# A causal mask folded into the row maximum on VectorE, cosine tables on ScalarE's queue, and the first rows normalized on ScalarE

## The chip, the cores and the metric

The kernel runs on one core of a Trainium2 chip. The metric is the device time of one execution in microseconds; the figure given is the median of three runs. Each core has five engines that run side by side and wait for each other by semaphores: TensorE (matmuls and transposes), VectorE, ScalarE, GpSimd, and SyncE, which here only issues transfers.

## The reference

One transformer block in float32 over 2048 rows of 1024 columns: attention with 16 heads of 64 columns and rotary positions, then a gated feed-forward part of 2752 columns whose weights are 4-bit codes with a scale per block of 64. Each part is wrapped in layer norms on both sides:

```python
x = x + layernorm(attn(layernorm(x), Wq, Wk, Wv, Wo))
x = x + layernorm(ffn(layernorm(x), gate, up, down))

# in attn, for each head
q, k = rotary(h @ Wq), rotary(h @ Wk)
logits = q @ k.T
logits = where(causal, logits, -1e9) / sqrt(64)
out = softmax(logits) @ (h @ Wv)

# in ffn
down(silu(gate(h)) * up(h))
```

## The kernel before

**Precision.** A float32 operand of a matmul is carried as a high part and a low part. `split` (L119) makes them: ScalarE casts the high part (L120), VectorE subtracts it from the source for the low part (L121). A product of two split operands is three matmuls (`mm3`, L114 to L116).

**First stage (make_x, prep_w, qkv).** `make_x` (L188) loads 128 rows of x at a time, takes the row statistics on VectorE and GpSimd (L126 to L137), normalizes the rows on VectorE (L195), transposes them on TensorE (L151) and splits the result. Four such row blocks make one block of 512 rows, of which there are four (c = 0 to 3). `prep_w` loads a slice of 128 columns of a projection's weights and splits it: ScalarE casts (L178), and for the first two slices GpSimd scales and subtracts (L183, L184). `qkv(m, c, ...)` (L211) projects row block c onto column slice m, which holds two heads. It loads the cosine and sine table of the block (`tab`, L214), makes 24 matmuls each for query, key and value, and takes the result out of its PSUM bank with a ScalarE copy (L223, L233). A query or key then goes through the rotary step: a shuffle (L235) and a product with the cosines (L236) on VectorE, a product with the sines (L237) and a sum (L238) on GpSimd, a split (L120, L121) and a store. A value is transposed (L226), cast and subtracted in two halves (tile `vo`, L230) and stored. The first two slices for all four row blocks, eight calls, form the ramp: they have `ramp=True`; with the transposes of x they are what TensorE does before attention starts. The tables live in the SBUF slot `f4`, of which there are four and which weight tiles, rotary results and value tiles share.

**Attention (scores, weighted).** For each head and each block J of 512 queries, `scores` (L244) goes through four sub-blocks j of 128 query rows. For each it takes the keys in tiles of up to 512 columns. A tile of scores is two matmuls into one of three PSUM banks named S (L260, L262). The last tile of each sub-block holds the diagonal: it is 128, 256, 384 or 512 columns wide, and only its last 128 columns are cut by the mask. There a third matmul (L264) adds the mask: identity times a triangle of -1e9, both in bfloat16. VectorE then takes the negated row maximum (L266), and ScalarE the exponential with that as its bias, with the row sums (L267). Over the whole kernel there are 640 tiles, 256 of them with the diagonal. After every second sub-block the sums are combined on VectorE (L272 to L284), and GpSimd scales the probabilities (L289). `weighted` (L292) transposes the probabilities (L299), splits them and multiplies them by the values (L303, L304). The projections of the later heads (`group`, L363) are placed between the attention work of the earlier ones.

**The rest.** The output projection (L445 to L447), the first residual with its layer norms (`residual`, L450, whose `normalize` at L144 is a ScalarE activation), the gated feed-forward with weights looked up from the codes, and a down projection done in seven half-size products with a last layer norm (`finish`, L682).

**What sets the order.** A planner sorts the program's instructions onto the engines by its own estimate of their durations and by priorities; `early` (L323) raises the priority of the first weights and of the x blocks, and `pace` ties projections to points in the attention work. Each engine then runs its list strictly in order. A transfer is issued by an instruction in the list of the engine whose queue is used: `load` is SyncE's. It carries one of eight completion semaphores in turn, and waits until the transfer that used the same one before has landed, beside its own data waits. The PSUM banks are one F, three S, three T and one O.

Of the kernel before, what the change touches and what calls it, by code (L numbers as in the profile page):

```python
# [10 lines left out]
F32 = mybir.dt.float32  # L11
FR = mybir.dt.float32r
BF = mybir.dt.bfloat16
# [11 lines left out]
P = 128  # L25
# [32 lines left out]
def block_kernel(ctx, tc, x, wq, wk, wv, wo, gu_codes, gu_scales, d_codes, d_scales, cos_sin, out):  # L58
# [15 lines left out]
    def slot(tag, shape, dtype, name):  # L74
        assert int(np.prod(shape[1:])) * 4 <= SLOTS[tag][1] * 1024, (tag, shape)
        return sb.tile(shape, dtype, tag=tag, name=name, bufs=SLOTS[tag][0])
# [9 lines left out]

    ident = const.tile([P, P], F32, name="ident")
    make_identity(nc, ident)
    ident_b = const.tile([P, P], BF, name="ident_b")
    V.tensor_copy(ident_b, ident)  # L90
    mask_f = slot("t2", [P, P], F32, "mask_f")
    G.memset(mask_f, 0.0)

    G.affine_select(out=mask_f, in_=mask_f, compare_op=ALU.is_ge, fill=MASK, base=0, pattern=[[-1, P]], channel_multiplier=1)
    mask_b = const.tile([P, P], BF, name="mask_b")
    V.tensor_copy(mask_b, mask_f)
    nhalf = const.tile([P, 1], F32, name="nhalf")
    G.memset(nhalf, -0.5)
# [41 lines left out]
    def halves(row):  # L140
        return row[:, :512], row[:, 512:]
# [46 lines left out]
    def make_x(c):  # L188
        tiles = [slot(("pa", "xc", "hd", "xc")[c], [P, 2, 2, 512], FR, "xr") for _ in range(4)]
        for t in range(4):  # L190
            r = (4 * c + t) * P
            xt = slot("hd" if c == 0 or t == 3 else "pw", [P, E], F32, "xt")
            load(xt, x[r : r + P, :])
            mean, rs, _ = ln_stats(halves(xt))
            V.tensor_scalar(xt, xt, mean, rs, ALU.subtract, ALU.mult)  # L195
            transposed(xt, tiles, slice(t * P, (t + 1) * P))
        for kp in range(4):
            load(xd[c][:, kp], f32(tiles[kp]))
        return tiles
# [11 lines left out]
    def qkv(m, c, ws, xs, ramp=False, pace=None):  # L211
        cs = slice(c * 512, (c + 1) * 512)
        tab = slot("f4", [P, 2, 512], F32, "tab")
        load(tab, cos_sin[:, :, cs])  # L214
        for n, w in enumerate(ws):
            o = bank("S" if ramp and n != 1 else "F", "qkv")
            for k in range(KE):
                mm = mm3(o, w[k], xs[k // 2][:, :, k % 2, :], k == 0, k == KE - 1)
                if k == 0 and pace:
                    pace(mm, n)  # L220
            t1 = slot("t2", [P, 512], F32, "t1")
            if n == 2:
                A.copy(t1, o)  # L223
                pv = bank("F", "pv").rearrange("p (t n) -> p t n", t=4)
                for t in range(4):
                    T.transpose(pv[:, t, :], t1[:, t * P : (t + 1) * P], ident)  # L226
                vo = slot("f4", [P, 4, 2, 2, D], FR, "vo")
                src = pv.rearrange("p t (a d) -> p t a d", a=2)
                for a in range(2):
                    split(vo[:, :, a, 0, :], vo[:, :, a, 1, :], src[:, :, a, :])  # L230
                load(vs[m][cs].rearrange("(t p) a n -> p t (a n)", p=P), f32(vo.rearrange("p t a l d -> p t (a l d)")))
            else:
                A.copy(t1, o)  # L233
                sh = slot("t2", [P, 512], F32, "sh")
                V.stream_shuffle(sh, t1, [i ^ 1 for i in range(32)])  # L235
                V.tensor_tensor(t1, t1, tab[:, 0, :], ALU.mult)  # L236
                G.tensor_tensor(sh, sh, tab[:, 1, :], ALU.mult)  # L237
                G.tensor_tensor(t1, t1, sh, ALU.add)  # L238
                hl = slot("f4", [P, 2, 512], FR, "hl")
                split(hl[:, 0, :], hl[:, 1, :], t1)  # L240
                load((qs, ks)[n][m][:, :, cs], f32(hl))


    def scores(J, q, k, anchors):  # L244
# [3 lines left out]
        for j in range(4):  # L248
# [5 lines left out]
            for i in range(nh):  # L254
# [4 lines left out]
                s = bank("S", "s")[:, : e - b]  # L259
                mm = T.matmul(s, lhsT=q[:, 0, j * P : (j + 1) * P], rhs=k[:, b:e], start=True, stop=False)  # L260
                anchors.append(((anchors[-1][0] if anchors else 0) + e - b, mm))
                T.matmul(s, lhsT=q[:, 1, j * P : (j + 1) * P], rhs=k[:, b:e], start=False, stop=not diag)  # L262
                if diag:
                    T.matmul(s[:, e - b - P :], lhsT=ident_b, rhs=mask_b, start=False, stop=True)  # L264
                mx = mxs[:, j % BATCH, i : i + 1]
                V.tensor_reduce(mx, s, AX.X, ALU.max, negate=True)  # L266
                A.activation(prob[i][:, j, : e - b], s, AF.Exp, bias=mx, accum_out=sums[:, j % BATCH, i : i + 1])  # L267
            if j % BATCH < BATCH - 1:
                continue
            rc = small.tile([P, BATCH, 4], F32, tag="rc", name="rc")[:, :, :nh]  # L270
# [401 lines left out]
            t = slot(tag, [P, 4, 512], F32, name)  # L672
            quarter.setdefault(name, []).extend([t[:, i] for i in range(4)])

    early_stats = {}

    def stats_of(name, r):
        st = small.tile([P, 2, 6], F32, tag=f"st_{name}{r}", name="st", bufs=1)
        V.bn_stats(st[:, 0, :], quarter[name][r])
        early_stats[name, r] = st  # L680

    def finish(r, lower, known, fresh, xt):  # L682

        t = 8 * (r // 4) + 4 * lower + r % 4
        load(xt, x1d[t * P : (t + 1) * P, :])
        st = early_stats[known, r]
        known, fresh = quarter[known][r], quarter[fresh][r]
        V.bn_stats(st[:, 1, :], fresh)
        _, rs, nb = ln_rest(st)
        a, b = (slice(512, E), slice(0, 512)) if lower else (slice(0, 512), slice(512, E))  # L690
        A.activation(xt[:, b], xt[:, b], AF.Identity, bias=nb)
        A.activation(known, known, AF.Identity, bias=nb, scale=rs)
# [98 lines left out]
```

## Time and profile before

| what | us |
|---|---|
| median of 3 runs (3069.14 to 3074.55) | 3069.32 |
| the profiled execution, whole | 3075.66 |
| its span in the trace | 3073.8 |
| L264, mask matmuls, 256, busy | 59.8 |
| L266, row maxima, 640, busy | 380.0 |
| L267, exponentials, 640, busy | 400.9 |
| L236 and L237 waiting for a cosine table | 103.3 |

The busy times of a line are sums over its instructions; those of TensorE overlap each other, because a matmul starts before the one ahead of it has ended. The granted TensorE clock was 0.982 over the execution. In the lines of the profile that follow, each row has an engine, a source line, an operation, the tile written and the tile read, and the shapes. In the time line the first two numbers are the start and the length in us, and the bracket holds the idle time of the engine ahead of the instruction with what ended it. In the table of stages each engine has its busy time in the stretch. In the list of groups the numbers after the count are the busy time in us and the mean in ns, and after the second bar the idle time ahead. In the list of waits they are the total in us, the count and the longest.

### The profile page before, as it was taken

To read this page: it belongs to the slowest core of one execution; us is meant where nothing else is said; L and a number is where in the kernel's file an instruction comes from. 1 tells how busy PE (TensorE), PEld (TensorE's weight loads), DVE (VectorE), ACT (ScalarE), POOL (GpSimd) and SP (SyncE) were. 2 spreads that over 40 slices of the span, in tenths; PEclk is the share of its full clock that TensorE was granted. 3 is DMA by queue.
4 is the path that set the end of the run, shared out by engine and by line. 5 is a ranking of instruction groups with operands and counts; after the bars stand their busy time and mean duration, and the time that the engine had idled before them with its cause. 6 is when DMAs were issued, how large, how long until landed. Compare 5 with 4: busy or idle time off the path is not lost.

```text
span 3073.8 us, 42810 instructions
## 1 busy us (share of the span) xinstructions
PE 2958.1 (96%) x14424; PEld 2426.6 (79%) x14424; DVE 2045.6 (67%) x3920; ACT 1700.1 (55%) x3565; POOL 960.4 (31%) x1055
## 2 busy tenths in 40 slices
PE   7979999999999999999989999999999999999998
PEld 6868888787777787777778788888888888788886
DVE  7556778777777777777565577766666677344347
ACT  3246667676666666666554466555555566332234
POOL 5334444344434343445323112222112223100034
PEclk9989999999999999999999999999999999999999
DMA  8776665747656558463346444344334444644446
GB/s 307 259 223 219 225 217 170 221 151 194 188 182 186 152 199 260 132 198 108 114 152 209 138 143 148 132 136 142 120 133 137 136 153 148 237 140 151 147 141 229
DMA packets 271739, 536.02 MB, mean 174 GB/s; under 512 B 22944, under 2 KB 113056, under 8 KB 255648
## 3 DMA queue, kind: packets, MB, share of 16 engines
q1 hardware_dynamic: 271520, 533.29, 53.8%
q8 instruction: 114, 1.87, 0.2%
q14 instruction: 105, 0.86, 0.1%
HBM read 371.98 MB, written 161.22 MB: 173 GB/s over the span
## 4 chain that ended last, share of the span: by engine, by line
PE 83%; DMA 8%; DVE 4%; ACT 2%; issue 1%; POOL 1%; SPq 1%; POOLq 0%; ACTq 0%; DVEq 0%
PE bk L114 14%; PE bk L115 14%; PE bk L116 14%; PE pt L299 6%; PE qkv L114 6%; PE qkv L115 5%; PE qkv L116 5%; PE o L304 4%; PE s L260 3%; PE o L303 3%; PE s L262 3%; DMA wf<-in_wq 1%; PE pj L445 1%; PE pj L447 1%; PE pj L446 1%
## 5 line engine op out<-in xcount | busy, mean ns | idle before, releaser
L115 PE MATMUL bk<-x,wt 128*128 128x512 f32 x1376 | 536.1, 390 | 0.0
L116 PE MATMUL bk<-x,wt 128*128 128x512 f32 x1376 | 535.8, 389 | 0.0
L114 PE MATMUL bk<-x,wt 128*128 128x512 f32 x1376 | 534.5, 390 | 0.9 <-ACT wt L120 0.9
L289 POOL TENSOR_SCALAR prob<-prob,rc 128x512 f32<-128x512 f32 (+3 forms) x640 | 405.4, 654 | 407.5 <-DVE rc L284 238.8
L267 ACT ACTIVATE prob<-s,mxs 128x512 f32<-128x512 f32 (+3 forms) x640 | 400.9, 629 | 159.1 <-DVE mxs L266 144.8
L121 DVE TENSOR_TENSOR pw<-pt,pw 128x512 fp32r<-128x512 f32 (+3 forms) x640 | 377.4, 602 | 131.2 <-ACT pw L120 129.5
L266 DVE TENSOR_REDUCE mxs<-s 128x1 f32<-128x512 f32 (+3 forms) x640 | 380.0, 602 | 100.5 <-PE s L262 60.2
L506 ACT ACTIVATE ln<-cs,bias 128x512 f32<-128x512 f32 x520 | 359.7, 716 | 109.4 <-DVE m L513 23.0
L120 ACT CAST pw<-pt 128x512 fp32r<-128x512 f32 (+3 forms) x640 | 323.1, 525 | 164.2 <-PE pt L299 134.9
L299 PE MATMUL pt<-ident,prob 128*128 128x128 f32 x2176 | 346.5, 276 | 3.2 <-DVE pw L121 3.0
L299 PEld LDWEIGHTS pt<-ident,prob 128*128 128x128 f32 x2176 | 267.9, 142 | 57.3 <-issue 4.4
L260 PE MATMUL s<-k,q 128*128 128x512 f32 (+3 forms) x640 | 268.7, 420 | 38.1 <-ACT prob L267 36.2
L114 PEld LDWEIGHTS bk<-x,wt 128*128 128x128 f32 x1376 | 258.8, 188 | 55.4 <-ACT wt L120 1.7
L116 PEld LDWEIGHTS bk<-x,wt 128*128 128x128 f32 x1376 | 258.5, 188 | 54.1 <-DVE wt L121 0.5
L115 PEld LDWEIGHTS bk<-x,wt 128*128 128x128 f32 x1376 | 258.6, 188 | 53.7
L304 PE MATMUL o<-pw,v 128*128 128x512 f32 (+3 forms) x640 | 250.3, 393 | 5.3 <-DVE pw L121 4.7
L303 PE MATMUL o<-pw,v 128*128 128x512 f32 (+3 forms) x640 | 246.7, 386 | 4.6 <-ACT pw L120 3.7
L114 PE MATMUL qkv<-xc,w 128*128 128x512 f32 x576 | 237.0, 411 | 13.6 <-ACT w L178 9.1
L114 PE MATMUL bk<-bt,at 128*128 128x512 f32 (+1 forms) x616 | 242.1, 395 | 4.3 <-ACT in L574 4.1
L115 PE MATMUL bk<-bt,at 128*128 128x512 f32 (+1 forms) x616 | 240.7, 391 | 0.0
L116 PE MATMUL bk<-bt,at 128*128 128x512 f32 (+1 forms) x616 | 239.8, 391 | 0.0
L262 PE MATMUL s<-k,q 128*128 128x512 f32 (+3 forms) x640 | 238.6, 374 | 0.0
(145 smaller groups left out, 5478.9 us busy)
## 6 DMA issues: line engine op xcount, KB each, us to landing
xc<-xd SPq DMA_DIRECT2D x96, 1024.0 KB, 8.9
q<-qs SPq DMA_DIRECT2D x128, 256.0 KB, 7.0
ast<-S SPq DMA_DIRECT2D x44, 512.0 KB, 4.0
cs<-in_gu_scales SPq DMA_DIRECT2D x172, 128.0 KB, 3.2
cs<-in_gu_codes SPq DMA_DIRECT2D x86, 256.0 KB, 2.9
A<-in SPq DMA_DIRECT2D x66, 256.0 KB, 2.1
S<-in SPq DMA_DIRECT2D x66, 256.0 KB, 3.1
ast<-A SPq DMA_DIRECT2D x33, 512.0 KB, 4.4
```

Of the source, the lines that this page charges most:

```text
L114: r = T.matmul(o, lhsT=w[:, 0], rhs=xx[:, 0], start=first, stop=False)
L115: T.matmul(o, lhsT=w[:, 0], rhs=xx[:, 1], start=False, stop=False)
L116: T.matmul(o, lhsT=w[:, 1], rhs=xx[:, 0], start=False, stop=last)
L121: V.tensor_tensor(lo, src, f32(hi), ALU.subtract)
L260: mm = T.matmul(s, lhsT=q[:, 0, j * P : (j + 1) * P], rhs=k[:, b:e], start=True, stop=False)
L266: V.tensor_reduce(mx, s, AX.X, ALU.max, negate=True)
L267: A.activation(prob[i][:, j, : e - b], s, AF.Exp, bias=mx, accum_out=sums[:, j % BATCH, i : i + 1])
L289: G.tensor_scalar(p, p, rc[:, jj % BATCH, i : i + 1], 0.0, ALU.mult, ALU.add)
L299: T.transpose(pt[:, j * P : (j + 1) * P], prob[kb // 4][:, j, kb % 4 * P : (kb % 4 + 1) * P], ident)
L303: T.matmul(o[:, cs], lhsT=v[:, kb, :], rhs=pw[:, 0, cs], start=kb == 0, stop=False)
L304: T.matmul(o[:, cs], lhsT=v[:, kb, :], rhs=pw[:, 1, cs], start=False, stop=kb == nk - 1)
L506: A.activation(ln, c8, AF.Prelu, bias=bias_of[ab], scale=ab[0], alpha=ab[2])
```

## The change

Three things change in the work, and one in where results are kept.

- The mask matmul of a diagonal tile goes. In its place one VectorE operation adds a mask of the tile's whole width to the scores, negates the sum, writes it back to the bank, and takes the minimum of the row, which is the negated maximum. The exponential of such a tile then has a scale of -1. The mask is 512 columns wide, and a tile of width w uses its last w columns; the bfloat16 identity is no longer needed.
- The eight cosine table loads of the ramp are issued on ScalarE's queue and not on SyncE's.
- The four row blocks of c = 0 are normalized by a ScalarE activation (L144 in the code before) and not on VectorE.
- The row statistics of the last stage lie in one tile for all rows, and not in one tile for each; the operations are the same.

```diff
-    ident_b = const.tile([P, P], BF, name="ident_b")
-    V.tensor_copy(ident_b, ident)
-    mask_f = slot("t2", [P, P], F32, "mask_f")
+    mask_f = slot("t2", [P, 512], F32, "mask_f")
     G.memset(mask_f, 0.0)
 
-    G.affine_select(out=mask_f, in_=mask_f, compare_op=ALU.is_ge, fill=MASK, base=0, pattern=[[-1, P]], channel_multiplier=1)
-    mask_b = const.tile([P, P], BF, name="mask_b")
+    G.affine_select(out=mask_f, in_=mask_f, compare_op=ALU.is_ge, fill=MASK, base=384, pattern=[[-1, 512]], channel_multiplier=1)
+    mask_b = const.tile([P, 512], BF, name="mask_b")
     V.tensor_copy(mask_b, mask_f)
...
-            mean, rs, _ = ln_stats(halves(xt))
-            V.tensor_scalar(xt, xt, mean, rs, ALU.subtract, ALU.mult)
+            stats = ln_stats(halves(xt))
+            if c == 0:
+                normalize(xt, xt, stats)
+            else:
+                V.tensor_scalar(xt, xt, stats[0], stats[1], ALU.subtract, ALU.mult)
...
-        load(tab, cos_sin[:, :, cs])
+        (A.dma_start if ramp else load)(tab, cos_sin[:, :, cs])
...
-                T.matmul(s, lhsT=q[:, 1, j * P : (j + 1) * P], rhs=k[:, b:e], start=False, stop=not diag)
+                T.matmul(s, lhsT=q[:, 1, j * P : (j + 1) * P], rhs=k[:, b:e], start=False, stop=True)
+                mx = mxs[:, j % BATCH, i : i + 1]
                 if diag:
-                    T.matmul(s[:, e - b - P :], lhsT=ident_b, rhs=mask_b, start=False, stop=True)
-                mx = mxs[:, j % BATCH, i : i + 1]
-                V.tensor_reduce(mx, s, AX.X, ALU.max, negate=True)
-                A.activation(prob[i][:, j, : e - b], s, AF.Exp, bias=mx, accum_out=sums[:, j % BATCH, i : i + 1])
+
+                    V.tensor_tensor_reduce(s, s, mask_b[:, 512 - (e - b) :], -1.0, -MASK, ALU.add, ALU.min, mx)
+                else:
+                    V.tensor_reduce(mx, s, AX.X, ALU.max, negate=True)
+                sign = -1.0 if diag else 1.0
+                A.activation(prob[i][:, j, : e - b], s, AF.Exp, bias=mx, scale=sign, accum_out=sums[:, j % BATCH, i : i + 1])
...
-    early_stats = {}
+
+    parts_st = small.tile([P, 8, 3, 6], F32, tag="parts_st", name="parts_st", bufs=1)
 
     def stats_of(name, r):
-        st = small.tile([P, 2, 6], F32, tag=f"st_{name}{r}", name="st", bufs=1)
-        V.bn_stats(st[:, 0, :], quarter[name][r])
-        early_stats[name, r] = st
+        V.bn_stats(parts_st[:, r, 0 if name == "c" else 2], quarter[name][r])
...
-        st = early_stats[known, r]
-        V.bn_stats(st[:, 1, :], fresh)
-        _, rs, nb = ln_rest(st)
+        V.bn_stats(parts_st[:, r, 1], fresh)
+        _, rs, nb = ln_rest(parts_st[:, r, lower : lower + 2])
```

## The prediction

> **What bounds the kernel now.** I read the busy shares first, then the table by stage, then the time line and the waits where the stage table shows TensorE idle.
>
> ```profile
> PE 2958.1 (96%) x14424; PEld 2426.6 (79%) x14424; DVE 2045.6 (67%) x3920; ACT 1700.1 (55%) x3565; POOL 960.4 (31%) x1055
> ```
> ```profile
> core 0: us, PE busy (x) PEld busy (x) DVE busy (x) ACT busy (x) POOL busy (x), PEclk, DMA share, GB/s
> 0.00:25.00 25.00, 7.82 (x30) 5.84 (x31) 19.79 (x53) 11.15 (x26) 16.76 (x30) 1.00 1.00 308
> 80.00:160.00 80.00, 80.00 (x381) 66.49 (x380) 37.64 (x80) 20.78 (x49) 29.91 (x22) 1.00 0.71 249
> 160.00:240.00 80.00, 61.88 (x301) 49.60 (x300) 45.61 (x105) 40.43 (x108) 30.72 (x34) 0.87 0.78 237
> 400.00:700.00 300.00, 294.06 (x1631) 241.99 (x1630) 230.59 (x524) 204.28 (x536) 126.09 (x171) 0.98 0.58 183
> 1000.00:1300.00 300.00, 289.91 (x1597) 237.41 (x1596) 224.69 (x515) 199.45 (x528) 121.85 (x169) 0.98 0.59 186
> ```
>
> TensorE is the bound, in the attention stage too: 294 of 300 us, with VectorE at 230.6 of 300 (77%). The holes are in the first 25 us (7.82 busy) and between 160 and 240 (18 us idle, granted clock 0.87). TensorE's order from about 1660 us on is the same before and after the change, so only what comes ahead of it is in question. The hole after 160 us, in the time line:
>
> ```profile
> 166.23 10.85 SPq L321 DMA_DIRECT2D q<-qs  x4
> 177.78 0.62 SPq L214 DMA_DIRECT2D tab<-in_cos_sin  x1
> 187.74 0.69 DVE L236 TENSOR_TENSOR t<-t,tab 128x512 f32<-128x512 f32 x1 [18.14 <-DMA tab<-in_cos_sin]
> 188.34 1.15 DVE L266 TENSOR_REDUCE mxs<-s 128x1 f32<-128x384 f32 x2
> 189.66 0.79 PE L260 MATMUL s<-k,q 128*128 128x512 f32 x1 [13.98 <-ACT prob L267]
> ```
>
> The eighth cosine table waits on SyncE's queue behind four query loads; VectorE's rotary product (L236) waits 18.14 us for it; the row maxima stand behind that product in VectorE's order, the exponentials behind the maxima, and TensorE waits 13.98 us for a score bank.
>
> **The mask matmul (L264) goes.** Its price is not its busy time:
>
> ```profile
> 1398.81 0.34 PE L262 MATMUL s<-k,q 128*128 128x384 f32 x1
> 1398.99 0.23 PE L264 MATMUL s<-mask_b,ident_b 128*128 128x128 bf16 x1
> 1399.03 0.31 PE L304 MATMUL o<-pw,v 128*128 128x128 f32 x1
> ```
>
> By row it lasts 0.234 us, and 256 x 0.234 = 59.8 us; but the next matmul starts 0.04 us after it. TensorE is freed of 256 x 0.04 = 10.2 us. Bounds: nothing (where TensorE waits anyway) to 10.2. TensorE is over 96% busy through most of the stage, so I take -10.2.
>
> **What VectorE takes on.** 256 of the 640 row maxima (L266) become an addition with a minimum reduction that also writes the negated, masked scores back to the bank, each followed by a second instruction that reads the accumulator out (the built program has both, 256 times). No row of the trace writes PSUM from VectorE or reads its accumulator. The nearest rows:
>
> ```profile
> L266 DVE TENSOR_REDUCE mxs<-s 128x1 f32<-128x512 f32 x448 | 303.3, 682 | 71.6 <-PE s L262 60.2 <-PE s L264 9.1
> L121 DVE TENSOR_TENSOR pw<-pt,pw 128x512 fp32r<-128x512 f32 x435 | 292.1, 682 | 95.3 <-ACT pw L120 94.1
> L267 ACT ACTIVATION_READ_ACCUMULATOR prob<-s,mxs 128x1 f32 x640 | 129.3, 202 | 0.0
> L137 DVE TENSOR_SCALAR nb<-mv,rs 128x1 f32<-128x1 f32 x6 | 1.2, 205 | 1.0 <-POOL rs L135 0.9
> ```
>
> A two-operand operation from a bank costs what the reduction costs (682 ns each at 512 columns), so the main instruction adds nothing at the low end; at the high end, writing the bank halves its rate, and it costs as much again (mean reduction over the four widths 679, 547, 415 and 282 ns: 0.48 us). I take nothing: the L121 row is the same form but for the place of its output. The read-out is between 0.10 us (ScalarE's lasts 202 ns, but half of it lies inside the activation before) and 0.205 us (L137, a one-column operation on VectorE); I take 0.15: 256 x 0.15 = 38 us of VectorE over the 1350 us from the first to the last of them, 2.8 points on 77%. Here a rule speaks against the change: the Trainium skill, "VectorE: DVE Perf Modes", sections "Two Vector instructions with no wait between them" and "Rules for kernel authors", says that an operation with an accumulator output is two instructions, and that one should save VectorE instructions, since each pays a fixed part. Its fixed part of 58 to 151 cycles at 0.96 GHz would make 0.06 to 0.16 us, an estimate from that page of 15 to 40 us; by the rows it is 26 to 52. Either fits under TensorE as long as VectorE is not the bound.
>
> What is exposed is latency. Who waits:
>
> ```profile
> PE s L260 <- ACT prob L267: 36.2, 18, 14.0
> ACT prob L267 <- DVE mxs L266: 144.8, 172, 13.9
> ```
>
> TensorE waits 18 times for an exponential, one of them the 14 us above. Three score banks lie between, and 256/640 = 0.4 of the tiles are diagonal: 17 x 3 x 0.4 x 0.15 = 3.1 us. I take +3.1. ScalarE's exponential only gets a scale of -1, which costs nothing.
>
> **The cosine tables on ScalarE's queue.** Eight loads leave SyncE. In the changed order each stands between the two halves of a value cast (L120, vo), and each waits for the transfers that used its completion semaphores before; while it waits, ScalarE is held. The first seven change nothing: from 40 to 160 us TensorE is 100% busy with tables arriving late, and ScalarE has 59 of 80 us to spare, against eight issues of 0.57 to 1.55 us on SyncE's row. The eighth decides. The half cast ahead of it is at 166.4. The issue then waits for a query load issued near 162.6, whose median landing is 7.9 us: 170.5. The table takes a median 9.7 us: 180.2. From landing to the matmul took 2.0 us (187.65 to 189.66): 182.2. That is 189.66 - 182.2 = 7.5 us earlier. Behind the waiting issue on ScalarE stand the first exponential and the other half cast, which frees the single F bank for the next key projection (168.6 in the trace): up to 3 us of new wait inside the same stretch. It also moves two masked maxima ahead of the rotary product on VectorE, which helps. Bounds: nothing (the next late thing is the second head's query load, held by TensorE itself) to 14 us, and a few more for the clock of 0.87. I take -7.5. The Trainium skill, "Trainium Kernel Development and Optimization", section "Key Constraints", has it that loads from other engines' queues run on the same DMA engines and save only the time to issue. By that rule the gain is 0.6 us, one issue, and the sum below is 6.9 us worse; by the row the table stood 10.85 us behind the four query loads, which waited for TensorE and not for bandwidth. I go by the row.
>
> **The first rows on ScalarE.** Four normalizations leave VectorE (L195, 0.8 to 1.6 us each) for ScalarE (L144, 1.24 us each at 128x1024, elsewhere in the trace). VectorE is 19.8 of 25 us busy there, ScalarE 11.2. But in the changed order ScalarE does the four, then six weight casts, and the last casts of the first row blocks come after the weight casts of the second group, whose wv load reaches ScalarE at 24.45. Four casts of 0.37 us later the last quarter of the first x tile is there: 24.45 + 1.15 + 1.5 = 27.1, where TensorE's first projection starts at 24.35 now. Some eight transposes are then already done (8 x 0.11 = 0.9). I take +1.5, between -2.5 (VectorE's two normalizations on the chain, 1.42 and 1.12 us, go) and +3.
>
> **The rest** costs nothing: a mask of 512 columns is built on GpSimd and cast on VectorE before the first row arrives (VectorE idles 2.38 us there; without it, about 1 us); the statistics of the last stage are the same count of instructions in one tile.
>
> **Sum**, against the profiled execution's own 3075.66 us (span 3073.8, 1.86 around it): -10.2 + 3.1 - 7.5 + 1.5 = -13.1, giving 3062.6. That execution is 6.3 us above the median of the runs, 3069.32, so the median should come to 3056. A planner that lays out the order from its own costs reorders all that comes ahead of 1660 us; for that I allow 6 us either way.
>
> **Rivals.**
> 1. *VectorE becomes the bound.* Place: the end of each of the 64 chunks (16 heads x 4 row blocks), where the last diagonal tile, its exponential, the reciprocal and GpSimd's scaling follow in series. If the main instruction runs at half rate, a tile costs 0.48 + 0.2 = 0.68 us more, VectorE rises by 256 x 0.68 = 174 us, to 90% of the stage, and one such tile exposed per chunk is 64 x 0.68 = 43.5 us. With the other terms (-10.2 - 7.5 + 1.5) the median is 3096.6; half exposed, 3075. It decides, against the 16.2 us gained, from 0.25 us exposed per chunk. For it: 172 waits of ScalarE for the maxima. Against: only 16.3 us of TensorE's waits for exponentials lie between 400 and 1300 us.
> 2. *The table was hidden anyway, or ScalarE is held.* The wait goes over to the second head's loads, or ScalarE's held queue gives the 7.5 back: -10.2 + 3.1 + 1.5 = -5.6, median 3063.7, no change that can be told. For it: loads behind the table were themselves held. Against: in the profile nothing but the table ends VectorE's 18.14 us.
> 3. *The mask is not worth 10 us*, since another engine ends each stall: the table's gain alone, -7.5 + 3.1 + 1.5 = -2.9, median 3066.4. Against it: the 96% and more.
>
> **From these to the numbers.** A measurement tells 0.2% (6.1 us) from no change: below 3063.2 is faster, above 3075.4 slower. The sum holds, with its spread: 0.58. Rivals 2 and 3, ending within 0.2%: 0.20. Rival 1, and ScalarE held long enough in the first stage, ending above: 0.22. The range reaches down to 3037 (the whole 14 us and the clock with it, the head 2.5 us better, the planner's 6) and up to 3083, which leaves out the outer part of rival 1. The likeliest case's own range is 3040 to 3063.
>
> **What would show it.** Right: no 14 us wait of L260 near 175 us, table landing near 180; the new VectorE instruction within 0.05 us of the reduction it replaces at each width, its read-out 0.1 to 0.2; VectorE near 80% in 400 to 700 and TensorE still above 97%; a first projection near 27 us. Wrong: the new instruction near 1.3 us at 512 columns, TensorE's waits for exponentials well above 40 us in total, or waits of TensorE for value casts behind ScalarE's loads.

## The result, and the profile after

| | before | after |
|---|---|---|
| median of 4 runs each (of before, the three given above and a fourth), us | 3071.94 (3069.14 to 3075.65) | 3042.42 (3042.17 to 3048.39) |
| ratio, with its 95% interval | 1 | 0.9913 (0.9893 to 0.9932) |
| the profiled execution, whole, us | 3075.66 | 3042.64 |
| its span in the trace, us | 3073.8 | 3040.9 |
| start of the first score matmul, us | 167.4 | 169.7 |
| start of the first score matmul of the last tile (the 1279th of 1280), us | 1515.4 | 1488.3 |
| start of the feed-forward part, us | 1680.7 | 1653.5 |

The changed kernel is 29.5 us faster by the medians. The two profiled executions differ by 33.0 us, and 27.2 of these are there when the feed-forward part starts. The rest lies in the part whose order the change doesn't touch; it takes 1387 to 1393 us in the traces of all the kernels here, with or without the mask matmul.

Line numbers have moved by a few: score matmuls are L261 and L263 now, the new operation is L267, the row maximum of the other tiles L269, the exponential L271, the transposes of the probabilities L303, the table load L215, the cosine product L237, the normalization on ScalarE L142.

The first two parts of the page of the changed kernel: the busy shares of the engines, and from the table of stages three of the stretches that were shown of before (busy time of each engine, then granted clock, DMA share and GB/s).

```profile
PE 2924.4 (96%) x14168; PEld 2411.7 (79%) x14168; DVE 2031.0 (67%) x4171; ACT 1698.5 (56%) x3569; POOL 955.7 (31%) x1055
```
```profile
core 0: us, PE busy (x) PEld busy (x) DVE busy (x) ACT busy (x) POOL busy (x), PEclk, DMA share, GB/s
0.00:25.00 25.00, 6.14 (x24) 4.57 (x24) 17.25 (x47) 14.87 (x26) 17.30 (x32) 1.00 1.01 315
160.00:240.00 80.00, 73.78 (x341) 59.08 (x340) 52.94 (x139) 47.73 (x127) 32.92 (x40) 0.89 0.84 267
400.00:700.00 300.00, 292.65 (x1611) 244.72 (x1610) 232.83 (x599) 208.46 (x552) 131.96 (x181) 0.99 0.61 190
```

The hole after 160 us has shrunk from 18.1 us of idle TensorE to 6.2. In the attention stage nothing has changed hands: TensorE is 292.7 of 300 us busy where it was 294.1, and VectorE 232.8 where it was 230.6, but more of the work is done in those 300 us. The first 25 us are worse (6.14 busy against 7.82).

The new VectorE operation, from the list of groups (after the bar: busy us, mean ns of one; after the second bar: idle time ahead). The second row is the read-out, the last is the reduction that it is to be held against:

```profile
L267 DVE CUSTOM_DVE_ANT_0 s<-s,mask_b 128x512 f32<-128x512 f32 x64 | 44.1, 689 | 4.9 <-PE s L263 3.4 <-ACT pw L118 1.2
L267 DVE DVE_READ_ACCUMULATOR2_ANT mxs<- 128x1 f32 x256 | 35.6, 139 | 0.0
L267 DVE CUSTOM_DVE_ANT_0 s<-s,mask_b 128x384 f32<-128x384 f32 x64 | 35.6, 556 | 5.3 <-PE s L263 4.6 <-ACT prob L271 0.2
L269 DVE TENSOR_REDUCE mxs<-s 128x1 f32<-128x512 f32 x384 | 260.8, 681 | 59.9 <-PE s L263 58.7
```

Writing the bank costs next to nothing (689 ns against 681), and the read-out 139 ns, with no idle time of VectorE ahead of any of the 256.

The eighth cosine table and the product that needs it, in the time line, and TensorE's waits for exponentials over the whole execution (total us, times, longest):

```profile
170.69 0.55 ACTq L215 DMA_DIRECT2D tab<-in_cos_sin  x1
...
181.50 0.69 DVE L237 TENSOR_TENSOR t<-t,tab 128x512 f32<-128x512 f32 x1 [5.86 <-DMA tab<-in_cos_sin]
```
```profile
PE s L261 <- ACT prob L271: 18.8, 29, 2.3
```

The table is asked for at 170.69 (177.78 before) and used at 181.50 (187.74 before); VectorE's wait for it went from 18.14 us to 5.86. The 14 us wait of TensorE is gone, and the longest is 2.3. There are more short ones: 29 for 18.8 us, where before 17 short ones made 22.2.

The first stage shows the cost of the third part of the change:

```profile
12.39 1.11 PE L149 MATMUL pt<-ident,xt 128*128 128x128 f32 x4 [0.50 <-ACT xt L142]
13.63 1.24 ACT L142 ACTIVATE xt<-xt,nb,rs 128x1024 f32<-128x1024 f32 x1
...
24.18 1.15 ACT L176 ACTIVATE w<-wf 128x512 fp32r<-128x512 f32 x2 [0.36 <-DMA wf<-in_wv]
26.44 2.79 PE L149 MATMUL pt<-ident,xt 128*128 128x128 f32 x12 [3.31 <-DVE xr L119]
28.88 1.63 PE L112 MATMUL qkv<-xr,w 128*128 128x512 f32 x3
```

The weight casts (L176) end at about 25.3, and the first projection (L112) starts at 28.88. It was 24.35 before. By the first score matmul 2.3 us of that 4.5 are left.

### The profile page after: what moved, and what is told of

Same layout as the page of the kernel before. It is cut to its first block, busy times and chain, and to the rows that moved or that the text cites. A ratio compares the mean times of both kernels' runs of the same rounds, so it can differ in the third digit from the quotient of the medians.

```text
span 3040.9 us, 42530 instructions
## 1 busy us (share of the span) xinstructions
PE 2924.4 (96%) x14168; PEld 2411.7 (79%) x14168; DVE 2031.0 (67%) x4171; ACT 1698.5 (56%) x3569; POOL 955.7 (31%) x1055
## 3 DMA queue, kind: packets, MB, share of 16 engines
q1 hardware_dynamic: 269344, 529.10, 53.5%
## 4 chain that ended last, share of the span: by engine, by line
PE 79%; DMA 9%; DVE 5%; ACT 3%; issue 2%; POOL 1%; SPq 1%; POOLq 0%; ACTq 0%; DVEq 0%
PE bk L112 14%; PE bk L113 14%; PE bk L114 14%; PE pt L303 6%; PE qkv L112 5%; PE qkv L114 5%; PE qkv L113 5%; PE o L308 4%; PE o L307 3%; PE s L261 3%; PE s L263 3%; DMA wf<-in_wq 2%; DMA q<-qs 1%; PE pj L451 1%; PE pj L449 1%
## 5 line engine op out<-in xcount | busy, mean ns | idle before, releaser
L112 PE MATMUL bk<-x,wt 128*128 128x512 f32 x1376 | 533.7, 389 | 1.0 <-ACT wt L118 1.0
L271 ACT ACTIVATE prob<-s,mxs 128x512 f32<-128x512 f32 (+3 forms) x640 | 402.1, 632 | 148.8 <-DVE mxs L269 92.1
L119 DVE TENSOR_TENSOR pw<-pt,pw 128x512 fp32r<-128x512 f32 (+3 forms) x640 | 378.4, 601 | 122.3 <-ACT pw L118 120.5
L303 PE MATMUL pt<-ident,prob 128*128 128x128 f32 x2176 | 345.8, 275 | 7.2 <-DVE pw L119 5.9
L303 PEld LDWEIGHTS pt<-ident,prob 128*128 128x128 f32 x2176 | 268.2, 142 | 61.7 <-issue 7.5
L112 PEld LDWEIGHTS bk<-x,wt 128*128 128x128 f32 x1376 | 258.2, 188 | 55.4 <-ACT wt L118 1.8
L269 DVE TENSOR_REDUCE mxs<-s 128x1 f32<-128x512 f32 x384 | 260.8, 681 | 59.9 <-PE s L263 58.7
L113 PEld LDWEIGHTS bk<-x,wt 128*128 128x128 f32 x1376 | 258.3, 188 | 53.5
L261 PE MATMUL s<-k,q 128*128 128x512 f32 (+3 forms) x640 | 266.2, 417 | 22.4 <-ACT prob L271 18.8
L112 PE MATMUL bk<-bt,at 128*128 128x512 f32 (+1 forms) x616 | 241.0, 393 | 3.7 <-ACT in L578 3.3
L112 PE MATMUL qkv<-xc,w 128*128 128x512 f32 x576 | 231.3, 402 | 13.3 <-ACT w L176 7.3
L263 PE MATMUL s<-k,q 128*128 128x512 f32 (+3 forms) x640 | 237.2, 373 | 0.0
```

The costliest lines, as they stand in the source:

```text
L112: r = T.matmul(o, lhsT=w[:, 0], rhs=xx[:, 0], start=first, stop=False)
L113: T.matmul(o, lhsT=w[:, 0], rhs=xx[:, 1], start=False, stop=False)
L119: V.tensor_tensor(lo, src, f32(hi), ALU.subtract)
L271: A.activation(prob[i][:, j, : e - b], s, AF.Exp, bias=mx, scale=sign, accum_out=sums[:, j % BATCH, i : i + 1])
L303: T.transpose(pt[:, j * P : (j + 1) * P], prob[kb // 4][:, j, kb % 4 * P : (kb % 4 + 1) * P], ident)
```

## The experiments

My theory after reading the result was that the mask matmul is worth about three times what I gave it. The rivals: the planner's new order is what is faster, the table's gain is larger than it looks, or VectorE took over something cheaply that was dear on TensorE. In all that follows a us figure that compares kernels of different chips is a difference of ratios to the kernel before, times 3073. "The attention stretch" is the time from the start of the 127th score matmul to that of the 1279th, in the profiled execution. It holds the same scores in every kernel, with 230 of the 256 diagonal tiles, and without the mask 6100 to 6125 matmuls (6100 before, 6104 after), as the order moves some of the other work over its ends.

### The three parts, one at a time

Each part alone on the kernel before, and the second and third together. The table alone:

```diff
-        load(tab, cos_sin[:, :, cs])
+        (A.dma_start if ramp else load)(tab, cos_sin[:, :, cs])
```

> The kernel before with the ramp's eight cosine loads on ScalarE's queue and nothing else. TensorE's order is the old one from its 764th instruction to the 803rd and from there to the end, so the planner takes no part. If the table's wait was worth what the milestones of the two traces show (12 us between the ramp's end and the 32nd score tile), the median falls by 12 us to about 3059. If the forecast's term was right, by 7.5 to about 3063. If the wait only moves on to the second head's loads, there is no change.

Measured: 3068.41 us, ratio 0.9982 (0.9975 to 0.9989), 5.4 us faster. The forecast's term was -7.5. In the time line of this kernel the table is used at 182.26, but another wait has come up:

```profile
173.41 0.55 ACTq L214 DMA_DIRECT2D tab<-in_cos_sin  x1
174.00 0.37 ACT L120 CAST vo<-pv 128x256 fp32r<-128x256 f32 x1 [6.57 <-DMA k<-ks]
174.40 0.42 DVE L121 TENSOR_TENSOR vo<-pv,vo 128x256 fp32r<-128x256 f32 x1 [5.65 <-ACT vo L120]
174.97 0.77 PE L114 MATMUL qkv<-xr,w 128*128 128x512 f32 x1 [6.19 <-DVE vo L121]
...
182.26 0.69 DVE L236 TENSOR_TENSOR t<-t,tab 128x512 f32<-128x512 f32 x1 [6.30 <-DMA tab<-in_cos_sin]
```

This is the hold of the second rival: ScalarE idles 6.57 us until a key load has landed, the half cast of the values stands behind the table's issue, and TensorE waits 6.19 us for it. In the kernel with the whole change that wait isn't there (its longest in 160 to 200 us is 2.9).

The first rows on ScalarE alone:

```diff
-            mean, rs, _ = ln_stats(halves(xt))
-            V.tensor_scalar(xt, xt, mean, rs, ALU.subtract, ALU.mult)
+            stats = ln_stats(halves(xt))
+            if c == 0:
+                normalize(xt, xt, stats)
+            else:
+                V.tensor_scalar(xt, xt, stats[0], stats[1], ALU.subtract, ALU.mult)
```

> The kernel before with the first four row blocks normalized on ScalarE and nothing else. Parts theory: the first score tile comes 3 us later (2.7 in the traces) and nothing else moves, so +3 us. Planner theory: the order of all that comes ahead of the output projection is new, and the time moves by up to 10 us either way with the cold spells of the clock.

Measured: 3075.86 us, ratio 1.0011 (1.0001 to 1.0022): 3.4 us slower by the ratio, 2.1 by the medians. The first projection starts at 29.20, the first score matmul at 169.3 against 167.4.

The mask alone, that is the changed kernel with the other two parts undone (the last stage's statistics stay in one tile; the lines of the mask's edit that matter):

```diff
...
-                T.matmul(s, lhsT=q[:, 1, j * P : (j + 1) * P], rhs=k[:, b:e], start=False, stop=not diag)
+                T.matmul(s, lhsT=q[:, 1, j * P : (j + 1) * P], rhs=k[:, b:e], start=False, stop=True)
...
                 if diag:
-                    T.matmul(s[:, e - b - P :], lhsT=ident_b, rhs=mask_b, start=False, stop=True)
...
+                    V.tensor_tensor_reduce(s, s, mask_b[:, 512 - (e - b) :], -1.0, -MASK, ALU.add, ALU.min, mx)
+                else:
+                    V.tensor_reduce(mx, s, AX.X, ALU.max, negate=True)
...
```

> The change without the cosine loads and without the rows on ScalarE: the mask in VectorE's operation alone. Parts theory: the 17.5 us that the attention stage gains between the traces come with the mask, so -17 us, to about 3053, with the 14 us wait for the table still there. Planner theory: the mask itself is worth 10.2 us of TensorE less 3 of latency, -7, and the rest is scatter of the order, so anything between -15 and +1.

Measured: 3043.10 us, ratio 0.9896 (0.9881 to 0.9910), 32 us faster, more than any theory gave it. The mask alone is as fast as the whole change.

Table and rows, everything but the mask (the first two edits above together):

> The change with the mask undone: matmul and row maximum as before, cosine loads and first rows on ScalarE. Parts theory: -12 + 3 = -9 us, to about 3061, and the attention stage after its first 32 tiles takes as long as before. Planner theory: the attention stage differs from before by several us although nothing in it has changed.

Measured: 3068.43 us, ratio 0.9981 (0.9971 to 0.9990), 5.8 us faster. So some four fifths of the gain or more are the mask's, and what table and rows add to it can't be told in the total: 0.9896 without them, 0.9913 and 0.9917 in the two measurements of the whole change. The table's gain is there early on in the profiled executions: the 33rd score matmul starts at 206.0 us before, at 200.1 with the table alone, at 204.0 with the mask alone, and at 198.2 after.

The attention stretch says the same (the last column is the time in which a matmul runs while the profile shows a granted clock below the full one):

| attention stretch, us | length | TensorE idle | busy at a reduced clock |
|---|---|---|---|
| before | 1206.6 | 49.4 | 46.9 |
| table alone | 1204.9 | 47.3 | 47.0 |
| rows alone | 1206.1 | 48.0 | 34.7 |
| table and rows | 1207.2 | 53.5 | 39.0 |
| after | 1187.3 | 56.1 | 29.2 |
| mask alone | 1183.9 | 53.2 | 27.1 |

The four kernels with the mask matmul lie within 2.3 us of each other, and the two without it 18 to 23 us below them. The planner's order hardly makes this difference. By tiles and shapes the kernels of the table have three orders of TensorE in the stretch: one for before, table alone, and table and rows; one for rows alone; one for the two without the mask. Four more executions without the mask, of the kernels run last, have two further orders and took 1180.2 to 1186.9 us; the changed kernel itself, profiled twice, took 1187.3 and 1184.5. TensorE does not wait less without the mask, it waits some 5 us more. What has gone is in the matmuls themselves.

### Where the 20 us were: the matmul behind the mask

Here is a diagonal tile of the kernel before in the time line, TensorE only, with its weight loads (PEld) up to the first one behind the mask:

```profile
1002.69 0.40 PE L262 MATMUL s<-k,q 128*128 128x512 f32 x1
1002.92 0.10 PEld L264 LDWEIGHTS <-ident_b 128*128 128x128 bf16 x1 [0.27 <-issue]
1002.93 0.23 PE L264 MATMUL s<-mask_b,ident_b 128*128 128x128 bf16 x1
1002.93 0.20 PEld L114 LDWEIGHTS qkv<-xc,w 128*128 128x128 f32 x1
1002.97 0.48 PE L114 MATMUL qkv<-xc,w 128*128 128x512 f32 x1
1003.28 0.40 PE L115 MATMUL qkv<-xc,w 128*128 128x512 f32 x1
1003.52 0.40 PE L116 MATMUL qkv<-xc,w 128*128 128x512 f32 x1
```

And one of the kernel after, at nearly the same place:

```profile
1002.95 0.34 PE L263 MATMUL s<-k,q 128*128 128x384 f32 x1
1002.95 0.19 PEld L112 LDWEIGHTS qkv<-xc,w 128*128 128x128 f32 x1
1003.12 0.40 PE L112 MATMUL qkv<-xc,w 128*128 128x512 f32 x1
1003.36 0.39 PE L113 MATMUL qkv<-xc,w 128*128 128x512 f32 x1
```

The projection behind the mask starts 0.04 us after it, as I had read. But its own weight load, 0.20 us long, begins only when the mask matmul starts; the matmul is recorded as started at 1002.97, with its weights still to come for 0.16 us. It lasts 0.48 us where its like last 0.40, and the one behind it starts 0.31 us later where 0.23 to 0.24 is usual. In the kernel after, the load of L112 (1002.95 to 1003.14) lies under the 384 columns of L263.

To count all of it, I took the time from the start of the second score matmul of a tile to the start of the second matmul behind it (the mask matmul not counted), for tiles of like width and like successor, at the full clock (medians, ns; here the successors are 512-column projections):

| width of the diagonal tile | before | after | the mask's price |
|---|---|---|---|
| 128 | 470 | 396 | 74 |
| 256 | 476 | 351 | 125 |
| 384 | 533 | 406 | 127 |
| 512 | 593 | 463 | 130 |

Over 217 of the 256 places that have a like in the kernel after, the mean is 109 ns: 256 x 0.109 = 27.9 us. This is what "by places" means below; other ways of choosing the like places give 101 to 113 ns, so 26 to 29 us. (At 128 columns the price is lower, and there the score matmul itself seems too short to cover the load behind it: the projection behind it lasts 0.45 us in the kernel after, and 396 is more than the 351 of the wider tile.)

The test: put a matmul of the mask's form back into the kernel after, without the mask's work.

```diff
-                T.matmul(s, lhsT=q[:, 1, j * P : (j + 1) * P], rhs=k[:, b:e], start=False, stop=True)
+                T.matmul(s, lhsT=q[:, 1, j * P : (j + 1) * P], rhs=k[:, b:e], start=False, stop=not diag)
+                if diag:
+                    T.matmul(s[:, e - b - P :], lhsT=mask_b[:, :P], rhs=mask_b[:, :P], start=False, stop=True)
```

> The changed kernel with one more matmul behind the two score matmuls of each diagonal tile: bf16, 128x128, weights and moving data both a block of zeros of the mask, so the result stays the same and VectorE still does the masking. It prices the 256 mask matmuls by themselves. If each costs only the 0.04 us to the next start, as the forecast had it, the time rises by 10 us, to about 3053. If it also lengthens the matmul behind it, whose weights can't be loaded while so short a matmul runs (0.315 us against 0.23 from start to start at 512 columns), each costs 0.115 to 0.13 us, and the time rises by 29 to 33 us, to about 3073.

And the same with 8 columns of moving data:

```diff
-                    T.matmul(s[:, e - b - P :], lhsT=mask_b[:, :P], rhs=mask_b[:, :P], start=False, stop=True)
+                    T.matmul(s[:, e - b - 8 :], lhsT=mask_b[:, :P], rhs=mask_b[:, :8], start=False, stop=True)
```

> As the kernel with the matmul of zeros, but the moving data has 8 columns in place of 128, with the same 128x128 weights. If the price is the time in which the columns pass, it falls with the columns: 256 x 0.003 us, under 1 us, about 3043. If the price is the weights of the matmul behind it, which can be loaded only while this one runs, the price stays where it was or grows a little: 25 to 35 us, about 3070 to 3077.

Measured: 3064.46 us (ratio 0.9966, 0.9953 to 0.9978) with 128 columns, and 3062.96 us (0.9964, 0.9953 to 0.9974) with 8. Against the kernel after (0.9915, the mean of its two measurements) that is 16 and 15 us more by the ratios, 22 and 21 by the medians of the first measurement. One sixteenth of the columns costs the same within what these runs can tell: the columns are not what is paid for. The time line of the narrow one:

```profile
1068.18 0.28 PE L263 MATMUL s<-k,q 128*128 128x256 f32 x1
1068.30 0.10 PEld L265 LDWEIGHTS <-mask_b 128*128 128x128 bf16 x1
1068.31 0.18 PE L265 MATMUL s<-mask_b 128*128 128x8 bf16 x1
1068.31 0.20 PEld L114 LDWEIGHTS qkv<-xc,w 128*128 128x128 f32 x1
1068.35 0.48 PE L114 MATMUL qkv<-xc,w 128*128 128x512 f32 x1
1068.66 0.40 PE L112 MATMUL qkv<-xc,w 128*128 128x512 f32 x1
```

Again 0.04 us to the next start, 0.48 us for the next matmul, 0.31 us to the one after.

A rival is left: that the price comes from the change between bfloat16 and float32, since both test matmuls are bfloat16 like the mask. The kernel after speaks against it. Here a float32 transpose of 128 columns stands where the mask stood:

```profile
1006.74 0.27 PE L303 MATMUL pt<-ident,prob 128*128 128x128 f32 x1
1006.74 0.19 PEld L114 LDWEIGHTS qkv<-xc,w 128*128 128x128 f32 x1
1006.76 0.48 PE L114 MATMUL qkv<-xc,w 128*128 128x512 f32 x1
1007.08 0.39 PE L112 MATMUL qkv<-xc,w 128*128 128x512 f32 x1
```

The pattern is the same without any bfloat16. At the full clock and without a wait a 512-column matmul follows such a transpose in 425 places of that trace, and the medians are 0.028 us to its start, 0.477 us for its length and 0.315 us to the next one.

By places the matmul of zeros costs 105 ns with 128 columns and 104 ns with 8, where the mask cost 109. The total fell short of the expected 29 to 33 us, though. A part is known: with the matmul of zeros TensorE is idle 48.3 us in the stretch and not 56.1 (52.1 with the narrow one), so it also stands where TensorE would otherwise have waited. The reduced clock (busy 46.6 us with the matmul of zeros, 29.5 with the narrow one, 29.2 after) explains none of the shortfall. The rest stays open; the interval of the difference is some 7 us either way.

### VectorE's side

The kernel with the matmul of zeros does all that the kernel with table and rows does, in TensorE's work too, except for VectorE's new operation with its read-out. Its ratio is 0.9966 against 0.9981, with intervals that overlap, and the stretch is 1207.7 us long against 1207.2. The 38 us that VectorE took on cost nothing that can be measured; the comparison is good to about 5 us. Nor do the exponentials come later: in the tiles of 384 columns they start 1.98 us after the second score matmul in both kernels, in the mean (at 256 columns 2.36 without the new operation and 2.50 with it).

That doesn't mean VectorE has room. Here the old row maximum is done as well, ahead of the new operation:

```diff
                 if diag:
+                    V.tensor_reduce(mx, s, AX.X, ALU.max, negate=True)
                     V.tensor_tensor_reduce(s, s, mask_b[:, 512 - (e - b) :], -1.0, -MASK, ALU.add, ALU.min, mx)
```

> The changed kernel with the old row maximum done as well ahead of the new operation, on each of the 256 diagonal tiles (its result is overwritten). Each diagonal tile then costs VectorE 0.48 us more in the mean, 123 us in all, about what a new operation at half rate would have cost. By the forecast's first rival, one such tile exposed per chunk, 64 x 0.48 = 31 us more, about 3073, and TensorE falls below 95% busy between 400 and 700 us. By the forecast's own latency term (17 waits x 3 banks x 0.4 x 0.48) 10 us more, about 3052. If VectorE has room and the three score banks hide it all, within 3 us of the changed kernel.

Measured: 3111.55 us, ratio 1.0121 (1.0102 to 1.0140), 63 us more than the kernel after; twice the price of the first rival and six times that of the latency term. In the stretch TensorE's idle time goes from 56.1 to 95.8 us, and the time at a reduced clock from 29.2 to 66.2 (a 512-column projection then starts every 0.43 us and not every 0.23, so 37 us of it cost some 17). TensorE's waits for exponentials, and the stage, in this kernel:

```profile
PE s L261 <- ACT prob L271: 54.0, 61, 5.2
```
```profile
400.00:700.00 300.00, 281.38 (x1513) 231.69 (x1511) 244.53 (x635) 195.34 (x521) 120.25 (x172) 0.98 0.63 193
```

VectorE is at 244.5 of 300 us, not at 300: it is not full, it is late. The exponentials of the 384-column tiles start 3.46 us after the second score matmul in the mean, where they start 2.05 us after it in the kernel after.

And a small addition, of the read-out's own length, behind the new operation:

```diff
                     V.tensor_tensor_reduce(s, s, mask_b[:, 512 - (e - b) :], -1.0, -MASK, ALU.add, ALU.min, mx)
+                    V.tensor_scalar(mx, mx, 1.0, 0.0, ALU.mult, ALU.add)
```

> The changed kernel with one more one-column VectorE instruction between the new operation and the exponential of each diagonal tile (the maximum times 1 plus 0, so nothing of the result changes). By the row of another instruction of this form it takes 0.14 us, so VectorE gets 256 x 0.14 = 36 us more: the read-out of the change a second time. If the price goes in proportion to the kernel that does the old row maximum as well (123 us of VectorE, 63 us of time), 18 us more, about 3061. If a small addition is hidden better than a large one, as the forecast's latency term has it (17 x 3 x 0.4 x 0.14), 3 us more, about 3046.

Measured: 3078.61 us, ratio 1.0016 (1.0007 to 1.0026), 31 us more than the kernel after, for 36 us of VectorE. Neither expectation holds. The group's row has the duration right (0.14 us); the time line of VectorE shows what I had left out:

```profile
L268 DVE TENSOR_SCALAR mxs<-mxs 128x1 f32<-128x1 f32 x256 | 35.9, 144 | 1.6
```
```profile
1102.04 0.42 DVE L267 CUSTOM_DVE_ANT_0 s<-s,mask_b 128x256 f32<-128x256 f32 x1
1102.38 0.14 DVE L267 DVE_READ_ACCUMULATOR2_ANT mxs<- 128x1 f32 x1
1102.38 0.69 DVE L119 TENSOR_TENSOR pw<-pt,pw 128x512 fp32r<-128x512 f32 x1
1102.98 0.68 DVE L119 TENSOR_TENSOR hl<-t,hl 128x512 fp32r<-128x512 f32 x1
1103.58 0.15 DVE L268 TENSOR_SCALAR mxs<-mxs 128x1 f32<-128x1 f32 x1
```

An instruction of its own is placed by the planner like any other, and here two subtractions (L119) have got between it and the operation that it belongs to. The added instruction starts over 0.1 us after the read-out has ended at 194 of the 256 places, and 0.74 us after it in the mean; the exponential, which needs it, is held for that too and not for 0.14 us alone. In the tiles of 384 columns the exponential starts 2.80 us after the second score matmul in the mean, against 2.05 in the kernel after. That is 0.75 us later for a price of 31 us, where the old row maximum made it 1.41 us later for 63 (at 256 columns 0.86 and 1.31): in these two kernels the price goes with the lateness of the exponential and not with the time that VectorE is given (36 and 123 us). The read-out of the new operation follows it directly at all 256 places.

### Without the rows on ScalarE, and another order

The rows alone cost 2 to 3 us, so the change without them should beat the whole.

```diff
-            stats = ln_stats(halves(xt))
-            if c == 0:
-                normalize(xt, xt, stats)
-            else:
-                V.tensor_scalar(xt, xt, stats[0], stats[1], ALU.subtract, ALU.mult)
+            mean, rs, _ = ln_stats(halves(xt))
+            V.tensor_scalar(xt, xt, mean, rs, ALU.subtract, ALU.mult)
```

> The changed kernel with the first rows normalized on VectorE again, as before. The first rows on ScalarE, made alone, cost 2 to 3 us, and in the changed kernel the first projection starts 4.5 us later than before (28.88 against 24.35). If that is lost time that nothing gives back later, this kernel is 2 to 4.5 us faster than the changed one, 3038 to 3040 us where the changed one has 3042. If the late start is made up by the end of the first stage, it is within 1 us of the changed one.

Measured: 3039.46 us, ratio 0.9888 (0.9873 to 0.9903). It looked 3 to 8 us better, so it was run beside the changed kernel on one chip, with a third kernel in which only a constant of the planner differs:

```diff
-PACE = 0.85
+PACE = 0.86
```

> The changed kernel itself, once more, so that it and the next one are measured on one chip: 3042 to 3047 us, 0.991 of the kernel before.

> The changed kernel with the first rows on VectorE, beside the changed kernel on one chip. If its lead (3039.5 against 3042.4 on two chips) is the head of 2 to 4.5 us, it comes out 2 to 5 us below the changed kernel again. If it was the scatter between chips and runs, the two are within 1 us.

> The changed kernel with the planner's pace constant at 0.86 in place of 0.85, so that the written order of TensorE's work differs and nothing else. It shows how much an order alone moves the time: the forecast allowed 6 us either way, and the orders of three kernels with the mask matmul lay within 1.2 us of each other over the attention stretch. I expect 3 us at most either way; if it is more than that, the last few us of the comparison of the kernels are no finding.

Measured: the changed kernel 3043.87 us, 0.9917 (0.9898 to 0.9937); without the rows on ScalarE 3046.43 us, 0.9919 (0.9899 to 0.9938); the other constant 3038.63 us, 0.9897 (0.9879 to 0.9915). The lead of the kernel without the rows did not come again, and a change of order alone is worth about as much (5 us by the medians, with overlapping intervals). None of these is shown to beat the changed kernel. The rows' 2 to 3 us show only where they are the only change.

## Why the prediction was right, and too small

The direction was right, and 3042.4 lies in the range and near the lower end of the likeliest case's own, 3040 to 3063. The sum was less than half of what was measured. That the range still held the result is luck in part: it reached so far down by room for the table, the first rows and the planner's order, while the surplus came from the mask, which had been given no room above 10.2 us.

| step | forecast, us | measured, us |
|---|---|---|
| the mask matmul off TensorE | -10.2 | -27.9 by places |
| what VectorE takes on | +3.1 | not to be told from 0 |
| the eighth table on ScalarE's queue | -7.5 | -5.4 alone |
| the first rows on ScalarE | +1.5 | +2.1 to +3.4 alone |
| sum | -13.1 | -29.5 (the rows above add up to some -30 to -31, but they come from different kernels) |

**The step that failed** is "the next matmul starts 0.04 us after it. TensorE is freed of 256 x 0.04 = 10.2 us". The mechanism was right and the term was mis-sized, because the price was read from one gap. I rejected the busy row (59.8 us) as overlapped, rightly, and then took the gap to the next start for the whole price. The rest stands one row further down, in the length of the matmul behind the mask and in the gap after that. The bounds that I set, nothing to 10.2, had no room for it. The trace of before has the mask's own weight loads as a group (256 of 98 ns), and I costed no weight load at all. The Trainium skill, "TensorE: Matmul & The Clock Gate", section "Back-to-back issue gap", says that the spacing of matmuls in a stream follows from the weight loads and the matmuls together, and gives about 81 ns for 128 columns where the formula for a lone one gives 56. Taken as a price, 256 x 0.081 would have been an estimate of 20.7 us; the places show 0.109 us. The load behind the mask takes 0.20 us here, where the mask's own takes 0.10; that this makes the difference to the page's figure is not shown. No matmul of the trace confirms the 81 ns itself.

**VectorE's new operation** was right in both its parts: 689 ns against the reduction's 681 at 512 columns (forecast: nothing more), the read-out 139 ns (forecast 150). The 256 read-outs are 35.6 us of VectorE, inside the 26 to 52 of the rows and also inside the 15 to 40 that the prediction worked out from the Trainium skill. The rule cited there ("VectorE: DVE Perf Modes", section "Rules for kernel authors"), to save VectorE instructions, showed no price for the read-outs, and 31 us for the separate instruction. The stage's VectorE share is 232.8 of 300 us, 77.6%, not the forecast's near 80. The exposed latency of 3.1 us is not shown: the runs give no price above their 5 us. TensorE's idle time in the stretch is some 5 us longer without the mask matmul, but with the matmul of zeros and the same work on VectorE it is not (48.3 us, where table and rows have 53.5). Its reasoning, lateness times banks times the share of diagonal tiles, is not to be trusted: for the kernel that does the row maximum twice it gave 10 us where 63 were measured.

**The table** went as told, with the issue at 170.7 (forecast 170.5), the product at 181.5 (table landing at 180.2 by the forecast) and TensorE's 14 us wait gone. The gain of 7.5 was near: the table alone made 5.4, and beside the mask no run shows its share of the total. Alone, part of it is given back by the hold of ScalarE that the second rival described. The rule that the prediction cites from the Trainium skill ("Trainium Kernel Development and Optimization", section "Key Constraints"), that only the issue time is saved, by which the gain would have been 0.6 us, is not what happened: the table came 6.2 us sooner because it no longer stood behind loads that were waiting for TensorE.

**The first rows** were right in sign and low. The first projection starts at 28.88, not 27.1: the weight casts end near 25.3 (25.6 by the forecast), but TensorE then still waits for a subtraction of VectorE (3.31 us in all), and 12 transposes of 2.8 us follow from 26.44, of which the forecast took some eight as done by then.

**The rivals.** The first, VectorE as the bound, did not come about, because writing the bank isn't at half rate. Its price had been too low: 43.5 us for 0.68 us more per tile, where 0.48 us more cost 63. By that price the change would have lost if the rate had been halved (an estimate from that run). The second holds in the form of the hold of ScalarE, but only where the table is moved alone. The third, that the mask is not worth 10 us, is refuted: alone it makes 32.

**What stays open.** By places the mask's price in the stretch is 230 x 0.109 = 25 us; TensorE's longer idle time takes 5 of it, and 14 us less at a reduced clock would add some 6. That makes 26, and the stretch is 21 us shorter (means of the four and the two kernels of the table). The reduced clock can't be put down to the mask: the two kernels with a test matmul have 46.6 and 29.5 us of it. The matmul of zeros, too, came out some 5 to 10 us cheaper than its places add up to. And why the small separate instruction costs more per us of VectorE than the large one (31 for 36 against 63 for 123) is argued from its place in the order and from the exponentials' lateness, and not shown by a run in which it directly follows its operation.

## What to carry to other kernels

Price a short matmul by what changes up to the start of the second matmul behind it: its own columns may be free, and the weight load of its successor, for which it leaves no cover, is not. On an engine that feeds the bound engine through a few buffers, a busy share of 77% by itself says little about room: in these runs the price went with how much later the result came that the other engine needs, and a separate instruction is later by whatever the order puts ahead of it. An operation with an accumulator read-out kept the two together, and was the cheaper form here.

## What the runs showed of the hardware

- A matmul is recorded as started while its own weights are still loading. Behind a mask matmul a 512-column matmul starts after 0.04 us, lasts 0.48 us in place of 0.40, and the next starts 0.314 us later in place of 0.23. Behind a float32 transpose of 128 columns it is the same: 0.028, 0.48 and 0.315 us.
- A bfloat16 matmul of 128x128 weights costs the same with 8 moving columns as with 128: 104 and 105 ns by places, when it stands among float32 matmuls with weight loads of 0.19 to 0.20 us (the two kernels with a test matmul).
- A VectorE operation that adds two operands, reduces along the row and writes its result back to PSUM takes 689, 556, 427 and 294 ns at 512, 384, 256 and 128 columns, where the plain reduction takes 681, 547, 414 and 280 (the kernel that does the row maximum twice has both); the accumulator's read-out takes 139 ns more, and no instruction came between.
